# A four-layer graph network on one core: one visit per gathered block, a shorter lead, and the last visit of layers 1 and 2 moved behind the product

## The chip, the cores and the metric

The kernel runs on one core of a Trainium2 chip. Its engines work side by side, each through its own queue in order: TensorE (PE, with its weight loads listed as PEld), VectorE (DVE), ScalarE (ACT), GpSimd (POOL) and SyncE (SP), which here only issues transfers. The metric is the device time of one execution in microseconds; the time before is the median of three runs, 2129.72 us.

## The reference, cut to what matters

A graph of N = 6250 nodes and E = 100000 edges, sorted by destination; each node has C = 256 features.

```python
def agg(h):
    return jax.ops.segment_sum(h[src], dst, num_segments=N)
x0 = relu(layernorm(x))
for l in range(3):
    h = x + agg(x)
    h = relu(h @ W1s[l] + b1s[l]); h = relu(h @ W2s[l] + b2s[l])
    x = h @ W3s[l] + b3s[l]
h = x + agg(x)
h = relu(h @ cW1 + cb1); h = relu(h @ cW2 + cb2)      # 256 -> 256 -> 64
out = input + h @ cW3 + cb3                           # 64 -> 256
```

So there are four rounds of "add up the rows of all neighbours", each followed by a small network on every node. Layers 0 to 2 below are the loop, layer 3 is the last block.

## The kernel before, in words

**Data.** The nodes stand in 49 blocks of 128 (block 48 holds the rest). The first matrix of a layer is multiplied into the rows before they are added up, so each layer works on z = x W1. `XY` holds z of all 49 blocks in fast memory, as a rounded half and a remainder. A table in device memory (`tables[l]`) holds the same rows for gathering.

**Two ways of adding up.** For most destination blocks the kernel has a matrix of edge counts against all 49 source blocks and multiplies it with `XY`: the *product*. Layer 0 does this block by block (line 1588); layers 1 to 3 do it by *panels* of four blocks, 20 to 47, seven panels, in 49 steps of four matmuls each (line 1665), and one or two single blocks. One step takes a tile `a` of counts, cast from bytes by ACT and DVE in turn (line 1565) and kept in a ring. The other blocks (0 to 19 and 48, in layer 0 also 44 to 47, less those that the product does) are *gathered*: a block has 17 tiles of 128 edges, and for each tile POOL fetches the 128 source rows of 1 KB by an indirect transfer (`send`, line 1382, into the pool `gath`). TensorE adds them into the destinations with one-hot matrices (`add`, line 1419): four strips of 32 columns side by side, for each strip one edge tile. A strip needs six edge tiles, `c + 4 m` with c from -1 to 4, so a block takes six *rounds*. Now they are done in two *visits* of three rounds each, with 8 and 9 of the 17 tiles. The one-hot tile `hot` of the next visit is made by DVE (`one_hots`, line 1402) right after a visit. There are 23, 20, 20 and 19 gathered blocks in layers 0 to 3.

**Order of the work.** The program is written out in order by a planner. `tick` is called once a step (four matmuls); it runs what is due (`later`), then jobs with a window of steps, then one step of the *queue* of MLPs, first in, first out. An MLP has two steps on TensorE: `seconds` (line 1233) and `thirds` (line 1290). A step of the queue is done when a visit falls into its window or the window ends; MLPs marked `hurry` are done at once, and while one is in the queue the others ahead of it hurry too. `third` ends with `store`, which writes z to the next table and, when block and source are used up, into `XY` (`split`, or `reload` from the table). When all 49 blocks of a layer are stored, `layers[l + 1].begin()` starts the next layer's gathers.

**Pace.** The kernel keeps a clock of TensorE's planned time (`passed`, `clock`). `begin` spreads the gathers evenly between its own time and `end`, the estimated end of the layer's work (`work_of`) less TAIL; each gather waits for the matmul at which it is due. A visit is done when the clock reaches its due time (`meets`), or from eight steps before the end of the layer's product, at least four steps after the one before. LEAD = 21 us is how far the asking runs ahead.

**End of a layer.** The last panel is 44 to 47; while it runs, `XY` is used for the last time, source block after source block, in the order 0 to 48. Block 48, alone in its group, is the last visit; its MLP and that of 44 to 47 are hurried.

Of the kernel before, what the change touches and what calls it, by code (L numbers as in the profile page):

```python
# [396 lines left out]
def sorted_edges(  # L397
# [59 lines left out]
    ROUNDS = ((3, 1, -1), (0, 4, 2))  # L457
# [40 lines left out]
    rel = const.tile([P, left[NQ] // T, len(ROUNDS), 3, P // Q], BF16, name="rel")  # L498
# [118 lines left out]
    def look(pool):  # L617
# [214 lines left out]
        for t, o in ((fd, rel), (fs, idx)):  # L832
# [4 lines left out]
            if o is rel:  # L837
                v = ps[:, :left[NQ]].rearrange("p (b k) -> p b k", k=T)
                for i, rounds in enumerate(ROUNDS):
                    for c in rounds:  # L840
                        g = 1 if c < 0 else 0
                        nc.vector.tensor_scalar(o[:, :, i, (c - min(rounds)) // 2, g:],
                                                v[:, :, c + 4 * g:c + 13:4], -1.0, None, op0=OP.add)
            else:
                nc.vector.tensor_copy(o, ps[:, :left[NQ]])
# [118 lines left out]
    with tc.manual_schedule():  # L964
# [129 lines left out]

        fetched = [0]

        def fetch(l, p):
# [7 lines left out]
            at = pool.tile([P, 4, CH * P], U8, name="at", bufs=bufs)  # L1105
            nc.sync.dma_start(out=at[:, :m * n, :], in_=mats[p][:, c:c + m, :, :].rearrange(
# [53 lines left out]
        def split(j, m, z):  # L1160

            nc.scalar.copy(XY[:, j:j + m, :C], z[:, :m, :])
# [9 lines left out]
        def bring():  # L1172
            while wanted:
# [13 lines left out]
                def back(j=j, z=z, of=of):  # L1187
                    split(j, 1, z)
                    later(1, lambda: given(of))
# [17 lines left out]
        def mlp(l, b0, n, h1, hurry, far):  # L1207
# [71 lines left out]
            def third(i):  # L1279
# [21 lines left out]
                def store():  # L1301
# [3 lines left out]
                    if all((l, j) in used for j in blocks):  # L1305
                        split(b0 + i, m, z)
# [28 lines left out]
        class Gathered:  # L1335
            def __init__(self, l):
# [11 lines left out]
                self.rows, self.us = {}, []  # L1348
# [10 lines left out]
            def meets(self):  # L1359
# [38 lines left out]
            def one_hots(self, v):  # L1398
                g, rounds = self.visits[v]
                shape = [P, len(rounds), P // Q, Q]  # L1400
                self.hot = work.tile(shape, F32, name="hot", bufs=2)
# [6 lines left out]
            def add(self):  # L1408
# [4 lines left out]
                if v == 0:  # L1413
                    self.one_hots(0)
                end = rounds == ROUNDS[-1]
                for c in rounds:
                    for m in range(P // Q):
                        if c + 4 * m >= 0:
                            nc.tensor.matmul(  # L1419
                                self.sums[m * Q:(m + 1) * Q, :C],  # L1420
                                self.hot[:, (c - min(rounds)) // 2, m, :], self.rows[g, c + 4 * m],
# [3 lines left out]
                if self.done < self.n:  # L1425
                    self.one_hots(self.done)
# [62 lines left out]
        tails = [7] + [panels[-1][1]] * NLAYER  # L1489
# [17 lines left out]
        LEAD, TAIL = 21.0, 10.0  # L1507
        COLS, FULL32, TURN, VISIT, BUILD, BURST = 0.457e-3, 1.68e-3, 0.4, 1.7, 0.2, 0.3
# [5 lines left out]
        ready, ring = [PRE], {}  # L1514

# [55 lines left out]
        def product_by_node(l, bs, ps_a, us, beside):  # L1571
            begun.setdefault(l, clock[0])
            aggs = [ps_a.tile([P, W], F32, name="agg") for _ in bs]
            for j0, m in solo_parts if l else node_parts[pieces.index(bs)]:
                at = now[0]
                tick(layers[l])
                layers[l].advance()
# [7 lines left out]
                for j in range(j0, j0 + m):  # L1585
                    for i, agg in enumerate(aggs):
# [56 lines left out]
        def product(l, p, ps_a):  # L1643
# [10 lines left out]
            for j in range(NT):  # L1654
                u = now[0]
                tick(layers[l])
                layers[l].advance()
                if l == NLAYER and p == last and j == NT - 3:
                    bring_inputs(b0, n)
                prepare(u + 1 + AHEAD + 2)  # L1660
                a = ring.pop(u)
                for c in range(KC):
                    for half in range(2):
                        o = half * C + c * P
                        mm = nc.tensor.matmul(agg[c][:, :w], XY[:, j, o:o + P], a[:, :w],  # L1665
                                              start=(j == 0 and half == 0),
                                              stop=(j == NT - 1 and half == 1))
# [25 lines left out]
        with tc.tile_pool(name="hots", bufs=1) as hots, tc.tile_pool(  # L1693
# [9 lines left out]
            layers[0].send(layers[0].upto[1])  # L1703
# [85 lines left out]
```

## Time and profile before

| | |
|---|---|
| median of three runs | 2129.72 us (2128.97 to 2136.23) |
| profiled execution, its own time | 2135.8 us |
| span of its trace | 2134.0 us |
| busy: PE, PEld, DVE, ACT, POOL | 96%, 70%, 44%, 41%, 68% |
| gathers (L1382) | 1394, 995 ns each |
| product matmuls (L1665, L1588) | 4116 and 1470 |
| one-hot matmuls (L1419) | 3772, 256.0 us of PE |
| granted TensorE clock | 0.988 |

The span runs from the first to the last instruction. A row of a wait names the engine and line that stood idle, what it was released by, the sum in us, the count and the longest. A row of a stretch gives its bounds, its length, and the busy time of each engine with its count of instructions. A row of the timeline gives start and length, the engine, the line, output and inputs with their shapes, a count of merged instructions, and in brackets the idle time ahead of it. A row of the chain gives start, length and what the chain went through. An fp32 matmul shows as two instructions or more.

### The profile page before, as it was taken

How to read it: one execution, taken by the hardware profiler on the slowest of the kernel's cores; microseconds unless marked ns; L12 is line 12 of the kernel's file. 1: busy time of each engine (PE TensorE's matmuls, PEld its weight loads, DVE VectorE, ACT ScalarE, POOL GpSimd, SP SyncE). 2: the span in 40 equal slices, each digit the busy share in tenths (PEclk: the TensorE clock that was granted, in tenths of full speed). 3: DMA queues.
4: the chain of work that ended last, by engine and by line, in shares of the span. 5: the costliest groups of instructions: out<-in, count | busy, mean ns of one | idle time of the engine just before them, and what ended most of it. 6: DMA issues, size and time to landing. Idle time of an engine off the chain costs nothing.

```text
span 2134.0 us, 33393 instructions
## 1 busy us (share of the span) xinstructions
PE 2057.4 (96%) x12076; PEld 1487.8 (70%) x12076; DVE 937.7 (44%) x2192; ACT 864.3 (41%) x1775; POOL 1445.4 (68%) x1470
## 2 busy tenths in 40 slices
PE   4979999999999999999999999999999999999997
PEld 3756766667667777777776777777776777777675
DVE  7877867667673422222233322222233433333332
ACT  4856655556556522323232433222333432223231
POOL 2727777777774477777776377777776277777773
PEclk9979999999999999999999999999999999999999
DMA  5524545545455655455455554555456555556553
GB/s 157 176 98 139 162 142 153 158 140 164 150 158 152 213 163 155 153 181 164 142 186 167 173 160 148 173 165 169 146 168 195 170 172 181 184 180 194 183 160 119
DMA packets 184901, 347.61 MB, mean 163 GB/s; under 512 B 32446, under 2 KB 118496, under 8 KB 184726
## 3 DMA queue, kind: packets, MB, share of 16 engines
q0 software_dynamic: 68960, 185.41, 29.7%
q1 hardware_dynamic: 113838, 158.12, 22.3%
q8 instruction: 97, 1.59, 0.3%
q10 hardware_dynamic: 1928, 1.85, 0.3%
q14 instruction: 78, 0.64, 0.1%
HBM read 287.98 MB, written 57.26 MB: 162 GB/s over the span
## 4 chain that ended last, share of the span: by engine, by line
PE 88%; DVE 5%; DMA 4%; issue 1%; ACT 1%; POOL 1%; SPq 0%; DVEq 0%; POOLq 0%; ACTq 0%
PE agg L1665 43%; PE agg L1588 16%; PE sums L1419 11%; PE ps L1233 6%; PE ps L1290 6%; PE bp L1076 4%; DMA rows<-table,idx 3%; PE ps L1479 1%; POOL rows L1382 1%; DVE junk L695 1%; PE bp L920 1%; DVE hi L1035 1%; DVE at L1086 1%; PE ps L1245 0%; DMA table<-zs 0%
## 5 line engine op out<-in xcount | busy, mean ns | idle before, releaser
L1382 POOL DMA_INDIRECT rows<-table,idx x1394 | 1387.7, 995 | 611.4 <-issue 220.6
L1665 PE MATMUL agg<-a,XY 128*128 128x512 f32 x4116 | 982.8, 395 | 1.9 <-DVE clT L1600 1.9
L1665 PEld LDWEIGHTS agg<-a,XY 128*128 128x128 f32 x4116 | 764.6, 188 | 209.5 <-issue 45.8
L1565 ACT CAST a<-at 128x512 fp32r<-128x512 uint8 (+1 forms) x542 | 326.9, 616 | 576.9 <-PE agg L1665 543.9
L1565 DVE CAST a<-at 128x512 fp32r<-128x512 uint8 x543 | 242.7, 448 | 552.8 <-PE agg L1665 469.3
L1588 PE MATMUL agg<-XY,a 128*128 128x512 f32 x1470 | 404.9, 409 | 1.3 <-DVE un L1600 0.7
L1588 PEld LDWEIGHTS agg<-XY,a 128*128 128x128 f32 x1470 | 258.9, 189 | 53.7 <-issue 8.7
L1419 PE MATMUL sums<-rows,hot 128*32 128x256 f32 x3772 | 256.0, 385 | 16.2 <-DMA rows<-table,idx 15.0
L1419 PEld LDWEIGHTS sums<-rows,hot 128*32 128x32 f32 x3772 | 112.6, 109 | 142.6 <-issue 53.6
L1549 ACT CAST a<-at 128x512 fp32r<-128x512 uint8 (+2 forms) x362 | 196.7, 574 | 6.5 <-PE agg L1588 6.5
L1084 ACT CAST at<-bp 128x392 uint8<-128x392 f32 x240 | 116.6, 487 | 203.7 <-PE bp L1076 191.0
L1086 DVE CAST at<-bp 128x392 uint8<-128x392 f32 x240 | 135.1, 563 | 138.2 <-PE bp L1076 138.2
L1448 DVE TENSOR_TENSOR u<-u,sums 128x256 f32<-128x256 f32 x82 | 34.3, 419 | 241.8 <-PE agg L1665 226.9
L1076 PE MATMUL bp<-hi,lo 128*128 128x196 bf16 x960 | 127.5, 255 | 11.0 <-DVE hi L1035 10.7
L1290 PE MATMUL ps<-w,h 128*128 128x256 f32 x588 | 133.9, 379 | 1.4 <-ACT h L1236 0.9
L1233 PE MATMUL ps<-h,w 128*128 128x512 f32 (+3 forms) x332 | 133.9, 545 | 0.6 <-DVE zz L1298 0.6
L1035 DVE TENSOR_TENSOR hi<-cols,pairs 128x784 bf16<-128x784 bf16 x240 | 134.3, 560 | 0.0
L1076 PEld LDWEIGHTS <-lo 128*128 128x128 bf16 x960 | 70.6, 99 | 81.9 <-DVE hi L1035 27.8
L1290 PEld LDWEIGHTS ps<-w,h 128*128 128x128 f32 x588 | 111.1, 190 | 18.7 <-ACT h L1236 1.8
L1483 ACT ACTIVATE h<-ps,bias 128x256 f32<-128x256 f32 (+1 forms) x116 | 47.2, 464 | 154.9 <-PE ps L1479 154.9
L1298 DVE TENSOR_TENSOR zz<-ps,w 128x512 f32<-128x512 f32 (+1 forms) x75 | 50.1, 678 | 117.0 <-PE ps L1290 117.0
L1035 DVE TENSOR_TENSOR lo<-lanes,pairs 128x512 bf16<-128x512 bf16 x240 | 100.3, 418 | 1.3 <-ACT pairs L1030 1.3
(171 smaller groups left out, 989.7 us busy)
## 6 DMA issues: line engine op xcount, KB each, us to landing
at<-mat SPq DMA_DIRECT2D x151, 448.0 KB
mat<-at SPq DMA_DIRECT2D x30, 784.0 KB
rows<-table,idx POOLq DMA_INDIRECT x1394
table<-zz SPq DMA_DIRECT2D x72, 256.0 KB
back<-table SPq DMA_DIRECT2D x99, 128.0 KB
xs<-in_x_dram SPq DMA_DIRECT2D x8, 768.0 KB
table<-zs SPq DMA_DIRECT2D x24, 256.0 KB
out_dram<-zz SPq DMA_DIRECT2D x24, 256.0 KB
```

The lines of the kernel that those rows point to most:

```text
L1035: nc.vector.tensor_tensor(o.rearrange("p q (n t) -> p q n t", t=2), values.rearrange("p (n t) -> p n t", t=2)[:, None, :, :].to_broadcast( ...
L1076: mm = nc.tensor.matmul(bp[:, m * HW:(m + 1) * HW], lo[:, q + m, :], hi[:, q + m, :], start=True, stop=True)
L1084: nc.scalar.copy(o, v)
L1086: nc.vector.tensor_copy(o, v)
L1233: mm = nc.tensor.matmul(ps[:mp, :w], weights[l][0][:, c, i * P:i * P + mp], h1[:, c, :w], start=(c == 0), stop=(c == KC - 1))
L1290: mm = nc.tensor.matmul(o, h2[0][:, c, nodes], w3[:, c, :], start=(c == 0), stop=(c == KC - 1))
L1382: got = nc.gpsimd.indirect_dma_start(out=t, out_offset=None, in_=tables[self.l][:, :], in_offset=bass.IndirectOffsetOnAxis(ap=idx[:, o:o + ...
L1419: nc.tensor.matmul(self.sums[m * Q:(m + 1) * Q, :C], self.hot[:, (c - min(rounds)) // 2, m, :], self.rows[g, c + 4 * m], start=(c == ROUND ...
L1549: nc.scalar.copy(a[:, i * m * P:(i + 1) * m * P].rearrange("p (j d) -> p j d", j=m), counts[b][:, j:j + m, :])
L1565: cast(o, at[:, :, d:d + m * P])
L1588: mm = nc.tensor.matmul(agg, a[:, d:d + P], XY[:, j, :], start=(j == 0), stop=(j == NT - 1))
L1665: mm = nc.tensor.matmul(agg[c][:, :w], XY[:, j, o:o + P], a[:, :w], start=(j == 0 and half == 0), stop=(j == NT - 1 and half == 1))
```

## The change

1. The two visits of a block become one of six rounds. All 17 tiles are needed at once; `hot` holds six rounds and has one buffer in place of two; it is made four steps after the visit, not right behind it. The clock's charge is 3.0 us a visit in place of twice 1.7.
2. The lead is no longer 21 us: a gather is due MARGIN = 6 us, plus the tiles behind it, before its visit. In layer 0 eight gathers go out at the start, as before.
3. From layer 1 on there are 27 slots of rows, not 25, and the ring of cast tiles has one buffer less (8).
4. In layers 1 and 2 the planned end of the visits is 5 us after the estimated end of the work, not 10 us before it, and a visit is forced ten steps after the product's end, not eight before. While a layer's visits are not all done, its `tick` and `advance` go on in the next layer's product (`open_one`). The estimate of the work left over to the next layer counts block 48 too (`tails`).
5. The panels of layers 1 to 3 take the source blocks by chunks of seven in the order 0, 1, 3, 4, 5, 6, 2, so that blocks 14 to 20 come last and 42 to 48 before them. New assertions see to it that a source block is written before it is read.

```diff
-    ROUNDS = ((3, 1, -1), (0, 4, 2))
+    ROUNDS = ((3, 1, -1, 0, 4, 2),)
...
+        CHUNKS = [0, 1, 3, 4, 5, 6, 2]
...
+            c = CHUNKS[c] if m == 1 else c
             nc.sync.dma_start(out=at[:, :m * n, :], in_=mats[p][:, c:c + m, :, :].rearrange(
...
-                return now[0] >= ends[self.l] - 8 or clock[0] >= self.first + (
+                return now[0] >= ends[self.l] + LATE[self.l] or clock[0] >= self.first + (
                     self.upto[self.done + 1] - self.upto[1]) * self.pace
...
             def begin(self):
-                self.first = clock[0] + LEAD
-                self.end = begun[self.l] + work_of(self.l) - TAIL
-                self.pace = (self.end - self.first) / (self.upto[-1] - self.upto[1])
+                self.one_hots(0)
+                self.end = begun[self.l] + work_of(self.l) - TAIL[self.l]
+                self.pace = (self.end - clock[0] - MARGIN) / self.upto[-1]
+                self.lead = MARGIN + self.upto[1] * self.pace
+                self.first = clock[0] + self.lead
...
-                    self.send(int((clock[0] - self.first + LEAD) / self.pace) + 1)
+                    self.send(int((clock[0] - self.first + self.lead) / self.pace) + 1)
...
-                self.hot = work.tile(shape, F32, name="hot", bufs=2)
+                self.hot = work.tile(shape, F32, name="hot")
...
                 if self.done < self.n:
-                    self.one_hots(self.done)
+                    later(4, lambda v=self.done: self.one_hots(v))
...
-        tails = [7] + [panels[-1][1]] * NLAYER
+        tails = [7] + [panels[-1][1] + gone[-1][1]] * (NLAYER - 1) + [panels[-1][1]]
...
-        LEAD, TAIL = 21.0, 10.0
-        COLS, FULL32, TURN, VISIT, BUILD, BURST = 0.457e-3, 1.68e-3, 0.4, 1.7, 0.2, 0.3
+        MARGIN = 6.0
+        TAIL = [10.0] + [-5.0] * (NLAYER - 1) + [10.0]
+        LATE = [-8] + [10] * (NLAYER - 1) + [-8]
+        COLS, FULL32, TURN, VISIT, BUILD, BURST = 0.457e-3, 1.68e-3, 0.4, 3.0, 0.2, 0.3
...
+        def open_one(l):
+            g = layers[max(l - 1, 0)]
+            return g if g.done < g.n else layers[l]
...
-            for j in range(NT):
+            for at, j in enumerate(c * CH + i for c in CHUNKS for i in range(CH)):
                 u = now[0]
-                tick(layers[l])
-                layers[l].advance()
+                tick(open_one(l))
+                open_one(l).advance()
...
-            layers[0].send(layers[0].upto[1])
+            layers[0].send(8)
...
-        rings = ctx.enter_context(tc.tile_pool(name="rings2", bufs=AHEAD + 6))
+        rings = ctx.enter_context(tc.tile_pool(name="rings2", bufs=AHEAD + 5))
...
-        gath = ctx.enter_context(tc.tile_pool(name="gath2", bufs=25))
+        gath = ctx.enter_context(tc.tile_pool(name="gath2", bufs=27))
```

More of the change, by code (lines that the diff above doesn't have):

```diff
@@ L497, in sorted_edges @@
     idx = const.tile([P, left[NQ]], I32, name="idx")
-    rel = const.tile([P, left[NQ] // T, len(ROUNDS), 3, P // Q], BF16, name="rel")
+    rel = const.tile([P, left[NQ] // T, len(ROUNDS), len(ROUNDS[0]), P // Q], BF16, name="rel")
     colf = const.tile([P, P], F32, name="colf")
@@ L1093, in build @@
                     yield
+        CHUNKS = [0, 1, 3, 4, 5, 6, 2]
+        assert 4 // panels[0][1] == 1 and sorted(CHUNKS) == [*range(NT // CH)]
         fetched = [0]
@@ L1158, in sorted_edges, with split @@
         BACK = 3
-        def split(j, m, z):
+        fresh = set()
+        def split(l, j, m, z):
+            fresh.update((l + 1, k) for k in range(j, j + m))
             nc.scalar.copy(XY[:, j:j + m, :C], z[:, :m, :])
@@ L1420, in add @@
                                 self.sums[m * Q:(m + 1) * Q, :C],
[L1421 removed]
+                                self.hot[:, c - min(rounds), m, :], self.rows[g, c + 4 * m],
                                 start=(c == ROUNDS[0][0]), stop=(c == ROUNDS[-1][-1]))
@@ L1661, in product @@
                 a = ring.pop(u)
+                assert (l, j) in fresh, (l, j, now[0], ends[l - 1], [k for k in range(NT) if (l, k) not in fresh], len(queue), layers[l - 1].done)
                 for c in range(KC):
```

27 lines of the change are left out of this document (15 added, 12 removed).

## The prediction

> **What bounds the kernel now.** I read the page's header and busy shares first, then the busy time by layer, then who waits for rows, then the order of work around a layer's end.
>
> ```profile
> span 2134.0 us, 33393 instructions
> PE 2057.4 (96%) x12076; PEld 1487.8 (70%) x12076; DVE 937.7 (44%) x2192; ACT 864.3 (41%) x1775; POOL 1445.4 (68%) x1470
> L1382 POOL DMA_INDIRECT rows<-table,idx x1394 | 1387.7, 995 | 611.4 <-issue 220.6
> ```
>
> TensorE looks like the only limit, at 96%. The mean hides a second one. The same gather line, in three stretches from the first to the last gather of layers 1, 2 and 3:
>
> ```profile
> 719.25:1164.30 445.05, 337.66 (x340) 1.00 0.56 173
> 1205.70:1648.60 442.90, 334.25 (x340) 1.00 0.56 172
> 1686.76:2106.00 419.24, 321.07 (x323) 1.00 0.58 184
> ```
>
> One gather each 1.31, 1.30 and 1.30 us (length over count), of which 0.99 us is busy; the rest is mostly an issue gap of 0.30 us, so within a layer POOL hardly ever rests. It rests between layers, since a layer's gathers need every row of the table that the layer before writes. Layer 3 is the shortest for TensorE, and there the rows are late at many visits. The stretches 1187 to 1670 and 1670 to 2134 are layers 2 and 3; the indented row is the idle time of layer 3's visits:
>
> ```profile
> 1187.00:1670.00 483.00, 479.42 (x2688) 352.05 (x2689) 146.52 (x330) 154.43 (x284) 334.26 (x340) 1.00 0.54 167
> 1670.00:2134.00 464.00, 447.36 (x2613) 326.62 (x2611) 153.64 (x340) 138.00 (x254) 321.07 (x323) 0.99 0.55 174
>   DMA rows<-table,idx: 19.5, 22
> PEld sums L1419 <- DMA rows<-table,idx: 27.5, 27, 3.8
> ```
>
> So two different stages stand in a row: up to the start of layer 3's gathers TensorE sets the time, and from there POOL does. Layer 3 ends about 418 us (323 gathers) plus a tail after its first gather; the tail is what follows the last one:
>
> ```profile
> 2105.01 0.95 POOL L1382 DMA_INDIRECT rows<-table,idx  x1 [0.30 <-DMA rows<-table,idx]
> 2128.39 1.44 SPq L516 DMA_DIRECT2D out_dram<-zz  x2
> ```
>
> The question for this change is therefore one number: when does the first gather of layer 3 start, now 1686.76? Work that TensorE does for layer 3 before that moment is lost time, since it later waits for rows anyway.
>
> **Part A, the ends of layers 1 and 2.** Today block 48's last visit is forced eight steps before the end of the product, and TensorE stands in it:
>
> ```profile
> 1159.03 1.92 PE L1419 MATMUL sums<-rows,hot 128*32 128x256 f32 x26
> 1163.34 0.96 POOL L1382 DMA_INDIRECT rows<-table,idx  x1 [0.30 <-issue]
> 1169.22 3.78 PE L1665 MATMUL agg<-a,XY 128*128 128x512 f32 x8
> 1648.15 1.06 PE L1419 MATMUL sums<-rows,hot 128*32 128x256 f32 x14
> 1653.47 2.11 PE L1665 MATMUL agg<-a,XY 128*128 128x512 f32 x8
> ```
>
> Two visits take 10.19 us from 1159.03 and one takes 5.32 us from 1648.15. With 1.43 us for a visit (next rows) the waits are 10.19 - 2.86 = 7.3 and 5.32 - 1.43 = 3.9 us. With TAIL -5 and LATE +10 the visit comes after the product's end, when its rows are there. Gain: 11.2 us. What is late next is what hangs on block 48, part C.
>
> **Part B, one visit in place of two.** From the chain of work in layer 3, and an fp32 matmul step of the MLP:
>
> ```profile
> 1705.91 9.31 PE agg L1665 x40
> 1715.22 1.43 PE sums L1419 x24
> 1716.65 9.31 PE agg L1665 x40
> 1725.96 1.43 PE sums L1419 x22
> 1198.42 3.46 PE ps L1290 x16
> 1193.16 3.43 PE ps L1233 x8
> ```
>
> A 256-column fp32 pass takes 3.46 / 16 = 0.216 us. A visit of three rounds is 6 such passes, four strips of 32 columns side by side: 1.29 us, so 0.14 us of its 1.43 is the change from one kind of work to the other. Six rounds in one visit: 12 passes and one change, 2.73 us in place of 2.86. There are 23 + 20 + 20 = 63 blocks in layers 0 to 2: 63 x 0.14 = 8.8 us gained. In layer 3 (19 blocks) POOL sets the end and it gains nothing. If the 0.14 belongs to each round and not to the visit, the gain is 0; I take 8.8, since a 22- and a 24-matmul visit cost the same.
>
> **Part C, the hand-over to the next layer.** The next layer's gathers begin when all 49 blocks are stored. Steps below are of four matmuls, 9.31 / 10 = 0.93 us. Layer 2 now, from the MLP of blocks 16 to 19 on:
>
> ```profile
> 1655.64 3.60 PE L1233 MATMUL ps<-h,w 128*128 128x512 f32 x8
> 1661.85 3.40 PE L1290 MATMUL ps<-w,h 128*128 128x256 f32 x15
> 1669.70 0.69 ACT L1678 ACTIVATE h<-agg,bias 128x512 f32<-128x512 f32 x1 [2.85 <-PE agg L1665]
> 1679.09 3.62 PE L1290 MATMUL ps<-w,h 128*128 128x256 f32 x16
> 1686.76 0.95 POOL L1382 DMA_INDIRECT rows<-table,idx  x1 [38.22 <-DMA clT<-in_L_gnn_cW_dram]
> ```
>
> 17 us from the product's end to the first gather, with some seven steps of layer 3's product in it. After: visits stand one block apart, 17 gathers of 1.30 = 22 us, and the last is planned 5 us after the end of the layer's estimated work. That estimate includes the last visit and the MLP of blocks 16 to 19, which now both fall behind the product's end, so in TensorE's time the last visit stands 5 + 3.4 + 7.5 = 16 us behind it on the kernel's clock (which charges 3.0 and 0.4 for visit and turn; capped at ten steps), and block 18's about 6 us ahead of it. Block 18's results are turned nine steps later when no visit comes, so the MLP of 16 to 19 stands behind that of 44 to 47, and block 48's, in the same first-in-first-out queue, behind both. Walking the queue with its gaps (two steps between the halves of a hurried MLP, three or four after others) the store of block 48 falls 20 steps after the product's end. Sum from end to first gather: 20 x 0.93 = 18.6; MLPs of 44 to 47 and 16 to 19, 2 x 6.9 = 13.8; the visit 2.7; turns 1.0; block 48's MLP, a quarter of one, 1.7; the wait for the ReLU right behind the product, 1.2 (an estimate from the 0.69 us above and the matmul before it); and 3.3 from there to the first gather, as now (1679.09 + 3.46 + 0.93 to 1686.76). 42.3 us in place of 17.1. Of the 25.2 more, 11.5 is work taken from before the product's end (MLP of 16 to 19, visit, turns, a half of block 48's MLP); the loss is 13.7, that is 13 steps of layer 3's product too early. With another 1.2 for the ReLU in layer 1: 15 us lost. Layer 1's longer hand-over costs no more than that as long as POOL keeps up in layer 2. Bounds: 1 (as long as now) to 19 (four steps more).
>
> **Part D, the shorter lead.** Today rows are asked for 21 us ahead on the kernel's clock; then MARGIN is 6 us. The row tile needed first and asked for last is tile 15, two paces plus 6, some 8.7 us, before the visit. What a gather needs, from its start to the matmul that waits for it, and the first gather of layer 1:
>
> ```profile
> 1163.34 3.99 DMA rows<-table,idx
> 2013.09 7.09 DMA rows<-table,idx
> 719.25 3.53 POOL L1382 DMA_INDIRECT rows<-table,idx  x1 [44.08 <-DMA back<-table]
> ```
>
> 4.0 to 7.1 us, so 1.6 to 4.7 us are left for the queue on POOL, which is nearly always full. Shortages: layer 0's last visit is still forced eight steps early, by my count 5 us ahead of its plan: 3 us. Layer 1 begins with a gather of 3.53 us: 1 to 2. Layer 2's pace is POOL's own 1.30: 2 to 3. Jitter in layer 0: 1. Together 8 us. Nearest rows: 27.5 us of waits in today's 164 visits, 0.17 a visit, over 63 blocks 10.6; and the end where rows are always late, layer 3's 19.5 in 38 visits, 0.51, over 63 is 32. Below: 0. I take 8, near the first.
>
> [...]
>
> **At nothing.** The one-hot tile, written once per block and in one buffer: two of these now, at most 1.1 us together, four steps after a visit with about 15 steps to the next; uncovered it would be 1.1 us a block.
>
> ```profile
> L1402 DVE TENSOR_TENSOR hot<-colf,rel 128x384 f32<-128x384 f32 x164 | 90.0, 551 | 0.0
> L1565 ACT CAST a<-at 128x512 fp32r<-128x512 uint8 x521 | 316.6, 620 | 564.8 <-PE agg L1665 534.7 <-PE agg L1588 8.5 <-issue 6.1
> L1565 DVE CAST a<-at 128x512 fp32r<-128x512 uint8 x536 | 240.0, 449 | 546.7 <-PE agg L1665 466.1 <-PE agg L1588 35.6 <-ACT a L1565 34.5
> ```
>
> A ring of 8 instead of 9 cast tiles: the casts wait for TensorE, not the other way, and are asked for six steps (5.6 us) ahead; uncovered, 0.6 us a step. The order of chunks: the same loads on SP's queue, and the blocks that come late are used at steps 36 to 49 of the next panel, later than their store by 15 steps or more. Layer 3's part of the long visits: when tile 15 comes last all six rounds follow, 1.3 us more behind it and 1.3 less behind tile 16, about 0.5 us at the end; slots of rows are not the limit where POOL is behind.
>
> **Sum.** Gains A 11.2 + B 8.8 = 20.0; losses C 15.0 + D 8.0 = 23.0. Layer 3's gathers begin 3 us later, its 418 us and tail stay, plus 0.5: +3.5 us on 2134.0, or 0.16%. The profiled execution took 2135.8, 6 us above the median 2129.72; the difference is put on the median: 2133 us.
>
> **Rivals.**
> - Slower: the short lead. Every visit of layers 0 to 2 waits for its last rows. For it: the layer 3 rows, 0.51 us a visit, and a POOL without rest. Against: today's waits in layers 0 and 1 before the forced end, of which the longest is
>
> ```profile
> 975.80 1.02 PEld L1419 LDWEIGHTS sums<-rows,hot 128*32 128x32 f32 x24 [0.76 <-DMA rows<-table,idx]
> ```
>
>   0.76 us with the 0.3 that stands ahead of most visits. At 0.4 us a visit, 63 x 0.4 = 25 in place of 8: 2133 + 17 = 2150. It decides from 0.24 us a visit (15 us, when the total passes +0.5%, 10.6 us).
> - Faster: the hand-over stays short, because the MLP of 16 to 19 finds a place ahead of the product's end and block 48's follows at once, and rows come in time. C falls to 1, D to 3 or 8: 2114 to 2119, say 2117. For it: today's order, where that MLP runs at 1655.64 and 1661.85, ahead of the end. Against: the job's nine steps and the queue's order.
> - Slower: too few slots. A block needs 17 and there are 27, so 10 can be on their way, 13 us of POOL's work. [...] If POOL stood for each visit's 2.7 us in layer 2, where it has no slack, 20 x 2.7 = 54 us: 2187. Against, the pacing asks only five tiles ahead of a visit, so the slots rarely bind, and no run here shows POOL waiting for one.
>
> **How the numbers follow.** My case 0.47; short lead 0.24; short hand-over 0.24; slots 0.05. No change is within 0.5%, 2119 to 2140, about what a measurement of this kernel can tell. Faster 0.24, same 0.47, slower 0.29. My own case alone: C from 11 to 19, D from 3 to 14, 2124 to 2143. The range takes in the short hand-over with its lower bound of D (2114) and the short lead to 0.45 us a visit (2152); the slots are left out.
>
> **What would show it.** A: no wait of several us in a visit ahead of the ends of layers 1 and 2. B: 82 groups of 46 matmuls at L1419's successor, 2.7 us each. C: from the last panel's ReLU to the next layer's first gather some 43 us, with the MLPs in the order 44, 16, 48. D: waits for rows in layers 0 to 2 of 8 us in sum; more than 15 makes the slower rival right. Layer 3: gathers still 1.30 us apart from its first to its last; if they have gaps, the pacing or the slots hold POOL, and the sum is wrong. A hand-over below 35 us makes the faster rival right.

## The result and the profile after

The changed kernel takes 2132.7 us (median of 20 runs, 2128.75 to 2139.99), the kernel before 2132.12 us beside it (20 runs, 2127.09 to 2138.86). The ratio is 1.0004, 95% interval 0.9995 to 1.0013: no difference. The forecast of 2133 us and "no change" holds. Its steps do not all hold: two failed, in opposite directions. Layer 3's gathers begin 12.3 us earlier in the profile, where 3 us later was foreseen, and what follows them is 5.8 us longer, where 0.5 was. That the medians came out as foreseen is therefore luck.

The page's header and the two groups that matter, after:

```profile
span 2127.5 us, 33239 instructions
L1389 POOL DMA_INDIRECT rows<-table,idx x1394 | 1387.5, 995 | 599.2 <-issue 223.8
PEld sums L1428 <- DMA rows<-table,idx: 41.6, 28, 6.0
```

The profiled execution took 2129.3 us, that of before 2135.8. Neither stands at its median, so of the 6.5 us between the two spans most is the scatter of single executions (the medians differ by 0.6), and what is worth reading is where the stages differ by more than executions of one kernel do. The stages show best on POOL's line. First and last gather of layers 1, 2 and 3, after:

```profile
720.41 4.40 POOL L1389 DMA_INDIRECT rows<-table,idx  x1 [43.68 <-PE agg L1682]
1174.18 1.06 POOL L1389 DMA_INDIRECT rows<-table,idx  x1 [0.30 <-PE agg L1682]
1201.36 1.30 POOL L1389 DMA_INDIRECT rows<-table,idx  x1 [26.12 <-PE agg L1682]
1641.74 0.95 POOL L1389 DMA_INDIRECT rows<-table,idx  x1 [0.30 <-issue]
1674.50 0.95 POOL L1389 DMA_INDIRECT rows<-table,idx  x1 [31.82 <-PE agg L1682]
2092.61 0.97 POOL L1389 DMA_INDIRECT rows<-table,idx  x1 [0.31 <-issue]
```

The same moments as a table. "Chain" runs from the first to the last gather of a layer, "gap" from the last gather of a layer to the first of the next, "tail" from the last gather to the end of the span. The last three columns are experiments told of below, in us:

| | before | after | after, again | tail3 | turn_early | margin8 |
|---|---|---|---|---|---|---|
| layer 1's first gather at | 719.2 | 720.4 | 721.9 | 720.4 | 721.0 | 722.7 |
| chain of layer 1 | 444.1 | 453.8 | 454.3 | 453.5 | 453.8 | 451.2 |
| gap 1 to 2 | 42.4 | 27.2 | 27.2 | 27.2 | 25.8 | 28.7 |
| chain of layer 2 | 441.9 | 440.4 | 440.5 | 440.4 | 441.2 | 438.5 |
| gap 2 to 3 | 39.2 | 32.8 | 32.6 | 32.1 | 31.7 | 33.6 |
| chain of layer 3 | 418.2 | 418.1 | 421.0 | 419.6 | 418.6 | 416.2 |
| tail | 29.0 | 34.9 | 35.3 | 31.8 | 33.5 | 36.6 |

From before to after: +1.2 + 9.7 - 15.2 - 1.5 - 6.4 - 0.1 + 5.9 = -6.4 us, the 6.5 between the spans but for rounding. Two executions of the same kernel ("after" and "after, again") differ by 1.5 us at layer 1's start and 2.9 us in layer 3's chain, and by 0.5 us or less in the rest. So the gaps got 21.6 us shorter, layer 1's chain 9.7 us longer, and the tail 5.9 us longer. Layer 1's gathers are spread over a plan that ends 15 us later; they start 1.34 us apart, 1.31 before. The second execution, which stands near its median, is only 1.3 us shorter than before (layer 3's first gather 10.3 us earlier, the rest 9.0 us longer).

The end of layer 1 after the change, by the timeline: the last panel's ReLU, block 48's visit, the two products of the MLP of 16 to 19, the first product of block 48's MLP, and its store.

```profile
1160.53 0.69 ACT L1695 ACTIVATE h<-agg,bias 128x512 f32<-128x512 f32 x1 [3.91 <-PE agg L1682]
1177.03 2.80 PE L1428 MATMUL sums<-rows,hot 128*32 128x256 f32 x46
1179.75 2.13 PE L1682 MATMUL agg<-a,XY 128*128 128x512 f32 x8
1181.94 3.60 PE L1238 MATMUL ps<-h,w 128*128 128x512 f32 x8
1188.15 3.62 PE L1295 MATMUL ps<-w,h 128*128 128x256 f32 x16
1194.37 1.06 PE L1238 MATMUL ps<-h,w 128*128 128x128 f32 x8
1198.63 0.74 SPq L521 DMA_DIRECT2D table<-zz  x2
```

The visit has no wait in it, and 1177.03 to 1179.75 is 2.72 us. Its 23 one-hot matmuls in fp32 show as 46 instructions, two each. And the end of layer 2:

```profile
1637.96 0.70 ACT L1695 ACTIVATE h<-agg,bias 128x512 f32<-128x512 f32 x1
1642.50 0.63 PE L1428 MATMUL sums<-rows,hot 128*32 128x256 f32 x6
1644.84 2.78 PE L1428 MATMUL sums<-rows,hot 128*32 128x256 f32 x40 [1.71 <-DMA rows<-table,idx]
1650.66 3.62 PE L1295 MATMUL ps<-w,h 128*128 128x256 f32 x16
1656.85 3.60 PE L1238 MATMUL ps<-h,w 128*128 128x512 f32 x8
```

Here block 48's visit comes 4.5 us behind the ReLU, ahead of the second half of the MLP of 44 to 47 (1650.66), and not behind it as in layer 1.

### The profile page after: what moved, and what is told of

Read it like the earlier page. It is cut to its first block, busy times and chain, and to the rows that moved or that the text cites. A ratio compares the mean times of both kernels' runs of the same rounds, so it can differ in the third digit from the quotient of the medians.

```text
span 2127.5 us, 33239 instructions
## 1 busy us (share of the span) xinstructions
PE 2034.8 (96%) x12076; PEld 1497.1 (70%) x12076; DVE 934.3 (44%) x2110; ACT 865.1 (41%) x1775; POOL 1444.4 (68%) x1470
## 3 DMA queue, kind: packets, MB, share of 16 engines
q0 software_dynamic: 68960, 185.41, 29.9%
## 4 chain that ended last, share of the span: by engine, by line
PE 86%; DMA 4%; DVE 4%; issue 1%; ACT 1%; POOL 0%; DVEq 0%; SPq 0%; POOLq 0%; ACTq 0%
PE agg L1682 43%; PE agg L1604 14%; PE sums L1428 11%; PE ps L1295 6%; PE ps L1238 6%; DMA rows<-table,idx 4%; PE bp L1076 4%; PE ps L1488 1%; DVE hi L1035 1%; DVE at L1086 1%; DVE lo L1035 1%; PE ps L1250 1%; PE ps L1230 0%; PE bp L920 0%; DVE hot L1412 0%
## 5 line engine op out<-in xcount | busy, mean ns | idle before, releaser
L1428 PE MATMUL sums<-rows,hot 128*32 128x256 f32 x3772 | 247.6, 389 | 28.4 <-DMA rows<-table,idx 28.3
L1428 PEld LDWEIGHTS sums<-rows,hot 128*32 128x32 f32 x3772 | 123.6, 111 | 145.1 <-DMA rows<-table,idx 41.6
```

What stands on the lines that cost most here:

```text
L1428: nc.tensor.matmul(self.sums[m * Q:(m + 1) * Q, :C], self.hot[:, c - min(rounds), m, :], self.rows[g, c + 4 * m], start=(c == ROUNDS[0][0] ...
```

## The experiments

They ran in three sets on three chips. On the second chip the kernel before takes 2130.7 us; on the first it takes 2360.1 and on the third 2390.2. The result above and its profiles have the second chip's times and are read with it. Ratios are to the kernel before in the same set. What the traces show of the two slower chips is in the last part; the cause stays open.

**Set 1: which layer do the gathers bound?** Both kernels leave out the gathers of tile 16 of every block in one layer, 19 or 20 of them, and take tile 15's rows in their place; all of TensorE's work stays. l2_16 has a 2 for the 3.

```diff
+                    if self.l == 3 and k == T - 1:
+                        self.rows[g, k] = self.rows[g, k - 1]
+                        self.sent += 1
+                        continue
```

> In layer 3 alone the last of the 17 row tiles of each of the 19 blocks is not fetched (the tile before it stands in for it, so these edges add wrong rows); TensorE does the same work. Theory (from layer 3's first gather on, POOL's chain of 323 gathers sets the end): 19 x 1.30 = 25 us less, of which TensorE's own work may leave some 20: about 2110 us. Rival (TensorE, 96% busy, is the limit everywhere): under 5 us.

> The same in layer 2 alone, 20 gathers and 26 us of POOL's time less. Theory (up to layer 3's first gather TensorE sets the time, and the short lead costs layer 2 some 7 us of waits for rows): those waits go, and no more: about 2126 us. Rival (POOL's chain sets every layer): 20 us or more. Rival (the waits are paid back in layer 3 anyway): no change.

l3_16: 2346.22 us, ratio 0.993 (0.9905 to 0.9955). l2_16: 2352.69 us, ratio 0.9965 (0.9942 to 0.9988). Each is the other's control in the layer that it leaves whole. Stretches from layer 2's first gather to layer 3's, and from there to the end, first l3_16, then l2_16:

```profile
1327.00:1866.00 539.00, 506.71 (x2665) 361.42 (x2663) 141.31 (x309) 152.91 (x283) 333.05 (x340) 0.99 0.48 148
1866.00:2345.00 479.00, 449.20 (x2518) 317.38 (x2516) 134.90 (x290) 124.18 (x225) 298.53 (x304) 1.00 0.51 157
```

```profile
1331.00:1842.00 511.00, 490.75 (x2659) 357.36 (x2658) 140.93 (x306) 151.81 (x280) 315.23 (x320) 0.99 0.49 150
1842.00:2352.00 510.00, 460.95 (x2521) 323.13 (x2519) 136.82 (x291) 125.26 (x226) 318.42 (x323) 0.97 0.49 153
```

Layer 3 is 31 us shorter (510 to 479) without its 19 gathers, 1.6 us each. But layer 2 is also some 27 us shorter without its 20. So on this chip gathers cost time in both layers, and TensorE's count of matmuls alone does not set it. That POOL's chain sets it, as theory has it, is not what the traces show. The weight loads of layer 3's visits, with all gathers (l2_16, two rows) and without 19 of them (l3_16):

```profile
PEld sums L1432 <- issue: 75.3, 113, 2.0
PEld sums L1432 <- DMA rows<-table,idx: 4.5, 4, 2.3
PEld sums L1432 <- issue: 60.4, 106, 1.3
```

TensorE hardly waits for rows (4.5 us, and 0.8 in layer 2), while POOL's gaps of over 0.4 us between gathers come to 73 us in layer 3 and 83 in layer 2: here POOL waits for TensorE. What gets shorter is mostly TensorE's visits, from a visit's first matmul to the next other work: 127.1 to 108.3 us in layer 3, 115.7 to 93.3 in layer 2; in layer 3 the granted clock is also 1.00 for 0.97. Why fewer gathers shorten the visits is open. On the second chip it is the other way round: after the change the same gaps come to 0.8 us in layer 2 and 2.8 in layer 3, and in layer 3 TensorE waits 27.8 us for rows. The experiment was not made there.

The layers that the two kernels leave whole add up to the changed kernel on this chip: 1866.0 us up to layer 3's first gather (l3_16) and 509.6 from there (l2_16). That is an estimate of 2376 us, some 16 above the kernel before.

**Set 1 and 3: the late last visit.** no_late undoes it and keeps the rest; late_only is the reverse: the kernel before, with its two visits, LEAD 21, old pace and 25 slots, and the late visit and the order of chunks added. First the edit of no_late, then the core of late_only's, both cut:

```diff
-        CHUNKS = [0, 1, 3, 4, 5, 6, 2]
+        CHUNKS = [0, 1, 2, 3, 4, 5, 6]
...
-        tails = [7] + [panels[-1][1] + gone[-1][1]] * (NLAYER - 1) + [panels[-1][1]]
+        tails = [7] + [panels[-1][1]] * NLAYER
...
-        TAIL = [10.0] + [-5.0] * (NLAYER - 1) + [10.0]
-        LATE = [-8] + [10] * (NLAYER - 1) + [-8]
+        TAIL = [10.0] * (NLAYER + 1)
+        LATE = [-8] * (NLAYER + 1)
```

```diff
-    ROUNDS = ((3, 1, -1, 0, 4, 2),)
+    ROUNDS = ((3, 1, -1), (0, 4, 2))
...
+                self.first = clock[0] + LEAD
+                self.lead = LEAD
...
-                self.pace = (self.end - clock[0] - MARGIN) / self.upto[-1]
-                self.lead = MARGIN + self.upto[1] * self.pace
-                self.first = clock[0] + self.lead
+                self.pace = (self.end - self.first) / (self.upto[-1] - self.upto[1])
...
-        gath = ctx.enter_context(tc.tile_pool(name="gath2", bufs=27))
+        gath = ctx.enter_context(tc.tile_pool(name="gath2", bufs=25))
```

> The changed kernel without its late last visit: in layers 1 and 2 the last visit is planned 10 us ahead of the estimated end and forced eight steps before the product's end, the chunks are in their old order; one visit per block, the 6 us lead and 27 slots stay. Theory (the late visit gains 11 us of waits and loses some 9 us in a longer hand-over): the waits at the ends of layers 1 and 2 come back, longer than before the change since the lead is short, the hand-over is 17 to 20 us again: 2134 to 2142 us. Rival (the hand-over eats the whole gain): 2133 or less.

> The kernel before with the late last visit and the order of chunks alone: two visits per block, lead of 21 us, 25 slots. Theory (the single visit's gain of 9 us in layers 0 to 2 and the short lead's loss of about that cancel, and the longer tail of layer 3 comes with the single visit): no waits at the ends of layers 1 and 2, a hand-over of 36 to 41 us, layer 3 as before: 2124 to 2128 us. Rival (the late visit gains nothing by itself): 2132.

> The kernel of the run no_late again (the last visit of layers 1 and 2 forced eight steps before the product's end, chunks of nodes in order, as before the change; the long visits and the short lead kept), on another chip than the slow one of the first run. Theory 1 (the forced visit waits at the ends of layers 1 and 2, 11 us and a slower clock behind it, and now has a shorter lead too, 5 to 10 us more): 2140 to 2152 us, 0.4 to 1% above the kernel before, waits of 5 us or more in visits ahead of both ends. Rival (the 40 us of the slow chip were the chip's own): within 0.3% of the kernel before.

no_late: 2402.49 us, ratio 1.0167 (1.0144 to 1.019); on the third chip, as no_late_2, 2426.62 us, ratio 1.0154 (1.0123 to 1.0184). late_only: 2356.92 us, ratio 0.9979 (0.9963 to 0.9995). Both runs of no_late are far above what was expected; late_only's 0.2% is about what its theory named (2124 to 2128 us for 2132). The third chip was no faster than the first, so no_late_2 confirms the loss (42 and 36 us) but does not say what it would be on the second chip. Gaps on the first chip: no_late 40.6 and 40.7 us; late_only 29.9 and 38.2; l3_16, which keeps the whole change in layer 2, 26.9 and 34.3. So the late last visit shortens the gaps by some 14 and 6 us, as between before and after above. Block 48's visit in no_late_2, at the ends of layers 1 and 2:

```profile
1317.22 5.05 PE L1428 MATMUL sums<-rows,hot 128*32 128x256 f32 x40 [3.85 <-DMA rows<-table,idx]
1877.59 4.76 PE L1428 MATMUL sums<-rows,hot 128*32 128x256 f32 x40 [4.42 <-DMA rows<-table,idx]
```

The forced visit waits, and the 40 matmuls behind the wait take 4.8 to 5.1 us. The wait need not be why: on this chip whole visits without one have a median of 5.3 us. The kernel before has the same forced visit, so that no_late loses 36 to 42 us to it must come from the rest of the change; two_visits, below, points at the long visit.

**Set 2: three edits of the changed kernel, beside itself.**

> The changed kernel as it is, beside the three others on the same chip. All theories: within 0.3% of the kernel before; the next three runs are read against this one's time and trace. Its last visit stands 16 steps of product (64 matmuls) ahead of the last panel's end, its first gather of layer 3 comes some 36 us after the ReLU of layer 2's last panel.

2134.25 us, ratio 1.0013 (0.9999 to 1.0027).

```diff
-        TAIL = [10.0] + [-5.0] * (NLAYER - 1) + [10.0]
+        TAIL = [10.0] + [-5.0] * (NLAYER - 1) + [0.0]
```

> One number: layer 3's plan ends with its work and not 10 us ahead of it, so the last visits come later and fewer steps of product are left behind the last one. Theory 1 (layer 3 is bound by POOL's gathers, and the product left behind the last visit, 16 steps of 0.93 us in place of 9 before, is pure loss at the end): the last visit stands 5 to 10 steps later, the stretch after the last gather is 30 us or less in place of 34.9, and the time is 4 to 6 us (0.2 to 0.3%) below the control. Rival (TensorE's work in layer 3 sets the end by now, so a step moved ahead of the last visit only moves the last gathers later by as much): the stretch after the last gather gets shorter but the last gather comes later, and the time is within 1.5 us of the control.

2128.69 us, ratio 0.999 (0.9978 to 1.0001), 0.23% below the control, give or take 0.18% (the half intervals added as squares). The tail falls from 35.3 to 31.8 us, with 36 product matmuls behind the last visit in place of 64, as before the change, and the last gather does not come later (2093.1 for 2097.4). So theory 1 holds; the 30 us or less that it named is missed because the visit now waits for its last rows, and pays twice, 1.99 us of wait and 4.46 us for 40 matmuls that take 2.78 at the end of layer 2:

```profile
2094.73 4.46 PE L1428 MATMUL sums<-rows,hot 128*32 128x256 f32 x40 [1.99 <-DMA rows<-table,idx]
```

```diff
+                    hand = 0 < self.l < NLAYER and b == self.blocks[-2][0] and g == n - 1
-                        job(far - 2, far - 2 + SPAN, turn)
+                        job(3 if hand else far - 2, 3 if hand else far - 2 + SPAN, turn)
```

> In layers 1 and 2 the turn of blocks 16 to 19, and so their MLP, starts 3 steps after the visit of block 18 in place of 5 to 11, nothing else. Theory 1 (the hand-over delays layer 3's first gather by the work that stands between the product's end and it): the MLP of 16 to 19 moves ahead of the product's end or of the MLP of 44 to 47, the time from layer 2's last ReLU to layer 3's first gather falls by one MLP, about 7 us (36 to about 30), and the kernel is 5 to 7 us (0.3%) faster than the control. Rival (block 48's own path, visit, store and reload of its rows, sets the hand-over, and the MLP only changes places with it): the hand-over and the time stay within 1.5 us of the control.

2128.16 us, ratio 0.999 (0.9981 to 1.0), 0.23% (give or take 0.17%) below the control. But the trace doesn't show why: in layer 2 the order stays as it was, the time from the last ReLU to layer 3's first gather is 33.5 us for 36.4 where theory 1 had a fall of 7, the gaps are only 1.4 and 0.9 us shorter, and another 2.4 us of the profile's difference lie in layer 3's chain (418.6 for 421.0), which the edit doesn't touch and which the first profile of the changed kernel has as well (418.1). In layer 2 the rival's mechanism is the one seen, but the time falls by more than it allows; the gain beyond some 2 us stays open.

```diff
-        MARGIN = 6.0
+        MARGIN = 8.0
```

> The lead 2 us longer in all layers, MARGIN 8 in place of 6, nothing else. Theory 1 (the short lead costs what TensorE waits for rows in layers 0 to 2, some 10 us in the changed kernel, and each wait is shorter by what the lead is longer): these waits fall to 4 to 6 us, layer 3 begins 4 to 6 us earlier and the time is 4 to 6 us (0.2 to 0.3%) below the control. Rival (the waits are at visits for which POOL is behind its plan already, so that asking earlier makes no row come earlier; or the 27 slots hold POOL): waits in layers 0 to 2 stay at 8 to 11 us and the time is within 2 us of the control.

2130.85 us, ratio 0.9993 (0.9981 to 1.0005), 0.20% (give or take 0.18%) below the control. The waits for rows in layers 0 to 2 (weight loads), first the control, then margin8:

```profile
PEld sums L1428 <- DMA rows<-table,idx: 14.1, 14, 2.8
```

```profile
PEld sums L1428 <- DMA rows<-table,idx: 9.6, 12, 2.6
POOL rows L1389 <- PE sums L1428: 16.9, 12, 3.4
```

Waits fall by 4.5 us and the time by 3.4, nearly as theory 1 has it, but 9.6 us of waits are left, which is the rival's figure. The second row is the rival's too: POOL now waits 16.9 us (control: 3.3) for a visit to free a slot. The 27 slots begin to bind at this lead. So neither holds whole.

All three edits are read against one control. Against the ratio of the result above, 1.0004, they are 0.14, 0.14 and 0.11% lower, about as much as the noise of these differences (0.13 to 0.15%). Their gains in time are therefore weaker evidence than what their traces show.

**Set 3: the visits and the lead, on the third chip.**

```diff
-    ROUNDS = ((3, 1, -1, 0, 4, 2),)
+    ROUNDS = ((3, 1, -1), (0, 4, 2))
...
-                self.hot = work.tile(shape, F32, name="hot")
+                self.hot = work.tile(shape, F32, name="hot", bufs=2)
...
-                    later(4, lambda v=self.done: self.one_hots(v))
+                    self.one_hots(self.done)
```

> The changed kernel with part B alone undone: two visits of three rounds per block again, two one-hot tiles of half the size, 1.7 us a visit on the kernel's clock; the short lead, the 27 slots and the late last visit stay. Theory 1 (each visit costs 0.14 us for the change from one kind of work to the other): 63 more visits in layers 0 to 2, the first gather of layer 3 some 9 us later, the time 0.3 to 0.5% above the changed kernel, 2138 to 2144 us. Rival (the time belongs to the rounds, or the two short visits win it back because the first can run while the last rows are on their way): first gather of layer 3 within 3 us of the changed kernel's 1674 to 1676, waits for rows in layers 0 to 2 below its 14 us of weight loads, the time within 0.15%.

In two_visits the planner's charge for a visit is 1.7 us again. three_edits is the three edits of set 2 in one kernel.

> The three edits that each came out 3 to 6 us below the control together: layer 3's plan ends with its work, MARGIN 8, blocks 16 to 19 turned 3 steps after block 18's visit. If each removes its own loss (product behind layer 3's last visit 3.5 us, waits for rows in layers 0 to 2 4 us, the place of the MLP of 16 to 19 up to 6 us): 2118 to 2123 us, 0.35 to 0.6% below the kernel before. If what they gained was chance in the runs or the same microseconds twice: 2126 to 2131 us, within 0.2% of the kernel before.

```diff
-        MARGIN = 6.0
+        MARGIN = 2.0
```

> The lead 4 us shorter, MARGIN 2 in place of 6, nothing else. From 6 to 8 the waits for rows in layers 0 to 2 (weight loads) fell from 14 to 10 us. Theory 1 (at 6 most visits of layers 0 to 2 have their last row only just in time, by less than 4 us): most of the 63 visits wait, 0.5 to 1.5 us each, 30 to 90 us in all with the slower clock behind the longer ones, 2150 to 2200 us. Rival (the waits come where POOL is behind its plan, elsewhere rows come early enough): the waits grow by 8 us or less, 2136 to 2142 us.

two_visits: 2364.81 us, ratio 0.9906 (0.9881 to 0.993), faster than the kernel before. three_edits: 2411.93 us, ratio 1.0105 (1.0079 to 1.0132). margin2: 2450.16 us, ratio 1.0261 (1.0232 to 1.029). The changed kernel itself did not run on the first or third chip; three_edits, the nearest to it, stands in for it here.

Theory 1 of two_visits falls on this chip, and with the other sign than either theory gave: two visits are 47 us faster than three_edits with its long visits, although three_edits has the three edits besides. TensorE's weight loads in the visits that nothing released, two_visits and then three_edits:

```profile
PEld sums L1428 <- issue: 92.6, 208, 3.3
```

```profile
PEld sums L1428 <- issue: 190.5, 317, 2.0
```

On the second chip the control has 37.4 us. One long visit of three_edits by its weight loads, and a visit of two_visits:

```profile
1402.30 1.45 PEld L1428 LDWEIGHTS sums<-rows,hot 128*32 128x32 f32 x31 [0.33 <-issue]
1403.92 0.24 PEld L1428 LDWEIGHTS sums<-rows,hot 128*32 128x32 f32 x4 [0.18 <-issue]
1404.66 0.17 PEld L1428 LDWEIGHTS sums<-rows,hot 128*32 128x32 f32 x4 [0.50 <-issue]
1406.12 0.12 PEld L1428 LDWEIGHTS sums<-rows,hot 128*32 128x32 f32 x2 [1.29 <-issue]
1407.55 0.16 PEld L1428 LDWEIGHTS sums<-rows,hot 128*32 128x32 f32 x4 [1.30 <-issue]
1408.99 0.13 PEld L1428 LDWEIGHTS sums<-rows,hot 128*32 128x32 f32 x1 [1.28 <-issue]
1409.55 5.62 PEld L1683 LDWEIGHTS agg<-a,XY 128*128 128x128 f32 x21 [0.44 <-issue]
```

```profile
1419.98 1.50 PE L1428 MATMUL sums<-rows,hot 128*32 128x256 f32 x24
```

The first 31 loads come in 1.45 us, then a few at a time with up to 1.3 us between them: 7.25 us from 1402.30 to 1409.55. Over the visits of 46 matmuls in three_edits without a wait for rows, the median from a visit's first matmul to the next other work is 4.4 us (no_late_2: 5.3; the control on the second chip: 2.73, the shortest everywhere). For visits of 22 and 24 it is 1.43. All visits together, waits for rows included, take 399 us in three_edits and 335 in two_visits. Some of it moves elsewhere: the product's weight loads stand still with no releaser for 107.6 us in two_visits and 61.4 in three_edits. So on this chip a block costs more in one long visit than in two short ones, and that very likely carries the losses of no_late, no_late_2 and three_edits; no run changed the visits alone. Nor is length all: in layer 0 of three_edits the same long visits take 2.9 us each, in layers 1 to 3 5.6.

Whether the three edits add up is not settled: they stand on the long visit, which is what costs time here. Nor did two_visits, the fastest here, run on the second chip, so no version is shown to beat both kernels on every chip.

margin2 answers its question: waits for rows in layers 0 to 2, with three_edits' 8.1 us in 11 waits beside it:

```profile
PEld sums L1428 <- DMA rows<-table,idx: 73.9, 32, 6.7
```

32 waits in 63 visits, and the time is 38 us above three_edits. So theory 1: many visits that do not wait with the longer lead do wait with this one. (Set beside three_edits, which has MARGIN 8; the changed kernel's 6 lies between.) The short-lead rival of the prediction is real at this margin; at 6, the control on the second chip has 14 waits of 14.1 us in all.

## Why the prediction was right, point by point

**What bounds the kernel.** Layer 3's chain of 418 us stayed 418.1 (421.0 in the second execution), as said, and there TensorE waits for rows:

```profile
PEld sums L1428 <- DMA rows<-table,idx: 27.8, 14, 6.0
```

That TensorE sets layer 2 is not refuted: it is busy 468 of the 473 us and waits 8.9 for rows. But POOL has no slack left there either, 0.8 us of gaps over 0.4 us, with 9.2 before. Which of the two would give is not tested on the second chip. The number that was to decide, layer 3's first gather, came at 1674.50: 12.3 us earlier, not 3 later.

**A, the waits at the ends.** Right: in layer 1's last visit no wait is left, in layer 2's 1.71 us (its 7.3 and 3.9 us were 11.2). It left out that the matmuls behind a wait can run slower (10 of them in 1.92 us and in 1.05 before, last part).

**B, one visit for two.** Right on the second chip in its size: 2.72 us for the predicted 2.73. The visits of layers 1 and 2 took 126.4 us before and 117.3 after (from a visit's first matmul to the next other work, summed between the first gathers of layers 1 and 3), where 40 x 0.14 = 5.6 is B. That one long visit can take 4.4 us, as in three_edits on the third chip, was in none of the rivals.

**C, the hand-over.** This step failed: it was priced at 15 us lost, and the steps of product that were done too early cost 6.5. It foresaw 42.3 us from the last ReLU to the next layer's first gather. In layer 1 it measured 40.8 (1160.53 to 1201.36) and in the order foreseen. In layer 2 it measured 36.5 (1637.96 to 1674.50), where block 48's visit came 4.5 us after the ReLU and not behind the MLP of 44 to 47 (16 us were foreseen; it was 16.5 in layer 1). Both are above the 35 us below which the faster rival would have been right. The price was oversized by its number of steps: 13 steps of layer 3's product were to be done too early, and it was 7, by the counts of TensorE instructions between the first gathers of layers 1 and 3, before and after:

```profile
719.25:1686.76 967.51, 958.41 (x5350) 701.71 (x5349) 292.59 (x665) 309.40 (x573) 671.92 (x680) 1.00 0.54 166
```

```profile
720.41:1674.50 954.09, 948.83 (x5378) 711.79 (x5378) 296.61 (x636) 315.35 (x582) 676.90 (x680) 1.00 0.55 170
```

28 matmuls more, 7 steps, 6.5 us. The stretch was to grow by 2 us (-11.2 - 5.6 + 15 + 4) and shrank by 13.4. Of it, the visits are -9.1 and the steps +6.5; the remaining -10.8 lie in the product, MLPs and turns. By the sums from each matmul's start to the next, 2.5 are in the product, about what the slow stretch behind before's wait in layer 1 costs outside the visit (3.4 less 0.9, last part). 5.6 are in the MLPs and 2.7 in the turns; why is not shown. Seen from POOL it is simple: its hand-over, counted from the last gather, used to hold the wait, the rest of the product and the MLPs; now the product is over when the last gather comes.

**D, the shorter lead.** Undersized, within its bounds of 3 to 14: the visits of layer 0 cost 4.5 us over 23 x 2.72 (predicted 3 + 1), those of layers 1 and 2 8.5 us over 40 x 2.72 (before: 12.0 over 80 x 1.43, where A's waits are), so 13 us for the 8 taken, slow matmuls included. By the waits of the weight loads it is 13.8 us, under the 15 that would have made the slower rival right. The lower bound of 3 us, which the forecast's range and its faster rival use, is layer 0's end alone, an estimate of the author's; no run of the changed kernel shows it, and its two executions have 13.8 and 14.1 us of waits.

**The tail.** This step failed too and hid the error of C: "its 418 us and tail stay, plus 0.5". The tail grew by 5.9 (6.3 in the second execution). Before, layer 3's last visit was due late and forced eight steps ahead of the end; after, it runs at its planned time, and 64 product matmuls stand behind it in place of 36. Its end, after:

```profile
2095.22 2.80 PE L1428 MATMUL sums<-rows,hot 128*32 128x256 f32 x46
2112.37 4.85 PE L1682 MATMUL agg<-a,XY 128*128 128x512 f32 x20
```

tail3 shows it: one number in the plan gives 3.5 us of the tail back.

**At nothing.** The larger one-hot tile and the smaller ring show no wait of a us. Layer 3's one long gap in the gathers is 2.39 us, behind a wait for rows of 6.0 us.

## What to carry to other kernels

When an engine's chain of transfers has no slack within a stage, do the sum over its idle stretches between the stages, from its last transfer to its next first one. Look first whether it has none on that chip: POOL's gaps in layer 2 came to 0.8 us on one chip and 83 on another. Sums over another engine's work mix what is hidden with what is not. When a plan's charges or lead change, look at where the last item of the last stage lands: nothing behind it can hide what was put there. A right total does not vouch for its terms: here two wrong ones offset each other. And a gain that comes from packing short instructions more densely should be tried on more than one chip: a visit of 46 matmuls took 2.73 us on the second chip (control) and 4.4 on the third (three_edits).

## What the runs showed of the hardware

**Around a wait of 2 to 3 us TensorE's granted clock fell to 0.50 in some cases and not in others.** The rows of two stretches of 20 us and the matmuls behind the waits, before; first a case of layer 1, then one of layer 2:

```profile
1160.00:1180.00 20.00, 14.83 (x67) 8.54 (x60) 2.62 (x7) 5.14 (x12) 3.39 (x4) 0.83 0.24 70
1167.38 1.92 PE L1419 MATMUL sums<-rows,hot 128*32 128x256 f32 x10 [3.19 <-DMA rows<-table,idx]
1640.00:1660.00 20.00, 16.72 (x99) 10.69 (x98) 5.30 (x15) 5.94 (x14) 6.71 (x7) 1.00 0.46 133
1652.49 1.05 PE L1419 MATMUL sums<-rows,hot 128*32 128x256 f32 x10 [3.28 <-DMA rows<-table,idx]
```

In the first the granted clock is 0.83 over the 20 us, 0.50 from 1166.5 to 1173.0, and 20 x 0.17 = 3.4 us of full speed are lost: the 10 matmuls take 1.92 us, 0.9 more than the same 10 in the second, and the 8 product matmuls at 1169.22 in the prediction take 3.78, for 2.1 elsewhere. In the second, with an even longer wait (3.28 us for 3.19), the clock is 1.00 throughout. The same visit at the end of layer 0, after and in turn_early:

```profile
677.28 4.11 PE L1428 MATMUL sums<-rows,hot 128*32 128x256 f32 x40 [2.35 <-DMA rows<-table,idx]
677.87 2.78 PE L1428 MATMUL sums<-rows,hot 128*32 128x256 f32 x40 [2.40 <-DMA rows<-table,idx]
```

The granted clock from 675 to 695 us is 0.91 in the first and 1.00 in the second; in the first it is 1.00 up to 678.5, 1.2 us behind the end of the wait, and 0.50 from 679.0 to 681.4. The 40 matmuls take 4.11 us after 2.35 idle and 4.46 after 1.99 (tail3, 0.83 from 2091 to 2101), but 2.78 after 2.40, and 2.78 after 1.71. So the length of the wait alone does not decide: the clock was lowered around waits of 1.99, 2.35 and 3.19 us and not around 1.71, 2.40 and 3.28. What decides is not shown. The wait of 2.35 us cost 1.3 more than its length (4.11 less 2.78), which the prediction's prices for waits left out.

**The three chips of these runs differ by up to 12%, and not evenly.** The kernel before takes 2130.7, 2360.1 and 2390.2 us on three chips. On the slower two, TensorE's weight loads stand still longer with no releaser, in the visits (190.5 us in three_edits, 188.7 in l3_16, for 37.4 in the control) and in the build of the counts in layer 0:

```profile
PEld L1076 <- issue: 95.7, 186, 4.3
```

in three_edits, against 25.6 us in the control. The MLPs' loads, 0.43 us apart, hardly change (50.8 for 44.1). What the loads of the visits and of the build wait for is not shown: the long visit above has 31 loads in 1.45 us and then one to four every 0.7 to 1.5 us, with no releaser in the trace. The gathers may have a part in it: with 19 of them left out the visits of layer 3 stand still for 60.4 us (l3_16) for 75.3 (l2_16), and with 20 left out those of layer 2 for 43.5 (l2_16) for 64.5 (l3_16).
